# A graph-transformer kernel: transposes of late x at steps 7 and 8, the last layer's scale and shift in a chain of their own, a final norm moved behind step 29

## The chip, the cores and the metric

The kernel runs on one core of one Trainium2 chip. The metric is the device time in microseconds (us) of one execution. The times of the kernel before come from three runs, given as median with lowest and highest; the profile is one further execution with its own time. The engines are TensorE (PE, matmul; its weight loads are listed as PEld), VectorE (DVE), ScalarE (ACT), GpSimd (POOL), and SyncE (SP), which here issues most DMA transfers.

## The reference

The input x holds 16 batches of 1024 nodes with 128 features, and adj is one 1024 x 1024 matrix of zeros and ones, shared by all batches. Three transformer layers follow one another, each with 8 heads of 16 features:

```
scores = Q K^T / 4,  where adj == 0: -inf
x = layer_norm(x + softmax(scores) V Wo + bo) * ln1_g + ln1_b
x = layer_norm(x + relu(x W1 + b1) W2 + b2) * ln2_g + ln2_b
```

The last layer is a graph attention: h = x W, e[i, j] = leaky_relu(h_i . a_src + h_j . a_dst), set to -inf where adj is 0, a softmax over j, and out = layer_norm(softmax(e) h + x) * ln_gamma + ln_beta. So after the third layer's own norm and its ln2_g and ln2_b, x enters twice: through W into the nodes, and once more as the residual that the aggregation adds.

## The kernel before

**Blocks and steps.** A block is one layer of one batch. Batches are taken in groups of four (LANES): for each group all four batches' layer 0, then their layer 1, then their layer 2 (line 835), which gives 48 blocks. The last layer of a batch is no block; it runs as side work beside the blocks that follow the batch's layer 2. A block has 32 steps: two groups of heads, two halves of the queries, eight tiles of 128 keys. In this text 14.4 is step 4 of block 14. The five x buffers (four lanes and one) hold the batches in work.

**A step.** TensorE makes the scores of four heads, in two PSUM slots of 1024 columns (L545; three slots in turn). The first slot goes through ScalarE's exponential (L553) and is then multiplied by a 0/1 mask on GpSimd (L554). The second has a large negative mask added on VectorE (L557) and then goes through the exponential (L569). At the ten steps of BOTH_ON_DVE both slots take the second way. Four steps later (AHEAD) TensorE multiplies the result with v into the bank `acc` (L574). A pipeline of scores, mask, exponential and product thus runs through all 1536 steps without a break, and TensorE's order in it is fixed.

**Side work.** All else is cut into tasks: the projections of the next block (`proj_tasks`, L383, whose results ScalarE and VectorE split into two parts `hi` and `lo`, L473 to L478); the copies of these into the row layout `stack` (L530, by SP); the attention output, the norms and the two feed-forward products of the block that has just ended (`post_tasks`); the transposition of x for the next block; and `last_tasks`. For these matmuls and transposes there is a single PSUM bank, `t`.

`last_tasks` for one batch are: two transposes of x, scaled and shifted on the copy (`xt`); the node products and exponentials (`nodes`); the rows g_rows and h_rows, sent as 16 small copies by SP (`send_rows`); eight tiles of edge scores (`edges`, L769 and L774); eight aggregations (`aggregate`, L383 and L785), each with its statistics (bn_stats and bn_aggr), and with GpSimd's `normalise` after each four of them; ln_gamma and ln_beta for each half; and the two stores. The scale of x by ln2_g and its shift for the residual stand between the `nodes` tasks.

`normalise` on GpSimd is two small operations and a power on the variance (L435), then one operation per 128 rows (L441). A scale or shift of all of x by a row is one GpSimd operation over 128 x 1024 (L511, L515, L632, L798); one for half of it works on 128 x 512.

**Transposition of x.** Normally it goes by DMA (`moved`): VectorE transposes 32 x 32 blocks (L357) and SP sends them out and back (L361, L375). Where x isn't ready at step 22 of the block before, `transpose_x` with by_dma=False puts two transposes on TensorE (L345) into the next block's turn, as the tasks ("xP"). This is so for the layer-0 blocks whose x is loaded late (blocks 13 to 15, 25 to 27 and 37 to 39, whose transposes run one block earlier, and block 1). In both cases the scale and shift of x by the previous layer's norm and by `bo` follow as two GpSimd operations (in layer 0 only the shift).

**What sets the order.** Tasks stand in chains. A task has a gap to the one before it, in steps, or a step of its own from a table: AT gives the transposes' steps ("xP"), the projections' steps 5, 7, 9, 11, 17 and 19, and those of `post_tasks`. At each step `piece` goes through the chains, those with a table step first, and takes at most one task without a "*"; tasks with "*", which need no TensorE, may be taken besides. Signs such as "+x" and "-x" count buffers: a task is held until its buffer is free. `fetch`, the load of a new batch (L167, SP), needs an x buffer, which the second store of an earlier batch frees ("-x"). `need` and `need_if` run a chain forward at once when its result is asked for. TensorE, ScalarE and SP execute in the order in which the program is written; VectorE's and GpSimd's order is set by a scheduler, but `issue_after(behind["pool"])` keeps an operation behind the latest GpSimd mask.

Of the kernel before, what the change touches and what calls it, by code (L numbers as in the profile page):

```python
# [29 lines left out]
LANES = 4  # L30
FIRST = 1


AT = {"xP": (4, 6), "proj": (5, 7, 9, 11, 17, 19), "post": (13, 15, 17, 18, 21, 22, 22, 23, 24, 25, 27, 29, 31, 35, 38, 40)}
AT_V_LAST = (9, 11, 17, 19, 20, 21)
AT_FIRST = (12, 14, 16, 18, 20, 22)
T_AT = 22
STACK_AT = 24
AT_END = {3: (12, 21, 22, 24, 25, 26, 27, 28, 30, 31), 2: (8, 9, 13, 14, 15, 16, 17, 18, 20, 21)}
AHEAD = 4  # L40
BOTH_ON_DVE = (3, 7, 8, 15, 23, 24, 26, 28, 30, 31)
TILES = {"w": 8, "x": LANES + 1, "last": 2}
BLOCKED = -57344.0
# [76 lines left out]
def fast_path(ctx: ExitStack, tc: tile.TileContext, a: dict, out: bass.AP, flag):  # L120
# [18 lines left out]
    def bank():  # L139

        if head[0] or tail[0]:
            return slot()[:, :512]
        return psum.tile([P, 512], F32, tag="t", name="t", bufs=1)
# [197 lines left out]
    def transpose_half(dst, src, h, gain=None, bias=None):  # L341

        ps = bank()
        for t in range(4):
            nc.tensor.transpose(ps[:, t * P:(t + 1) * P], src[:, 4 * h + t, :], identf)  # L345
        dv, pv = dst.rearrange("p (j t e) -> p t j e", j=4, t=4), ps.rearrange("p (t j e) -> p t j e", j=4, t=4)
        with soon():
            if gain is None:
                nc.scalar.copy(dv, pv)
            else:  # L350
                nc.scalar.activation(dv, pv, AF.Identity, scale=gain, bias=bias)
# [72 lines left out]
    def normalise(n, ts):  # L424

        scalars(n, ts)
        subtract_scale(n, ts)
# [68 lines left out]
    def transpose_x(m, by_dma=True):  # L496
        b, l = blocks[m]
        x, xT = state["x", b], xt_tile("xT")
        state["xT", m] = xT
        if by_dma:  # L500
            put(moved(lambda: xT, lambda: x), ("xT", m))
        elif m == 0:
            for h in range(2):
                transpose_half(xT[:, h], x, h)
        else:
            put([(0, lambda: transpose_half(xT[:, 0], x, 0), ""), (0, lambda: transpose_half(xT[:, 1], x, 1), "")],
                ("xP", m), first=True)

        def scale():
            with tc.issue_after(behind["pool"]) if m else nullcontext():  # L510
                nc.gpsimd.tensor_mul(x, x, rows(W[l - 1]["ln2_g"]))  # L511

        def shift():
            with tc.issue_after(behind["pool"]) if m else nullcontext():
                nc.gpsimd.tensor_add(x, x, rows(W[l]["bo"]))  # L515
        if m:
            put(([(6, scale, "*")] if l else []) + [(2 if l else 6, shift, "*")], ("shifted", m))
        else:
            shift()

# [180 lines left out]
    def last_tasks(b):  # L701
# [3 lines left out]
        def xt(h):  # L705
            def run():
                w = W[L - 1]
                if h == 0:

                    s["col"] = work.tile([P, 4, NT], F32, tag="col", name="col", bufs=2)  # L710
                    s["hd"] = [work.tile([P, 4, D + 1], F32, tag="w", name="hd", bufs=TILES["w"]) for _ in range(2)]
                    s["n"] = with_stats(state["x", b])
                s["xT", h] = half_tile("xT")
                transpose_half(s["xT", h], state["x", b], h, w["ln2_gc"], w["ln2_bc"])
            return run

        def nodes(t0, t1):
            def run():
                col, ts = s["col"], slice(t0, t1)

                halves = [slice(max(t0, 4 * h), min(t1, 4 * h + 4)) for h in range(2)]
                halves = [(c, s["hd"][c.start // 4][:, c.start % 4:(c.stop - 1) % 4 + 1, :])
                          for c in halves if c.start < c.stop]
                ps = bank()
                for t in range(t0, t1):
                    by_columns(ps[:, (t - t0) * (D + 2):(t - t0 + 1) * (D + 2)],
                               s["xT", t // 4][:, t % 4 * P:(t % 4 + 1) * P], w_nodes)
                pv = ps[:, :(t1 - t0) * (D + 2)].rearrange("p (t d) -> p t d", d=D + 2)
                with soon():
                    nc.scalar.activation(col[:, 2, ts], pv[:, :, D + 1], AF.Exp, scale=NEG_SLOPE)  # L730
                    nc.scalar.activation(col[:, 0:2, ts].rearrange("p c t -> p t c"), pv[:, :, D:], AF.Exp,
                                         scale=1 - NEG_SLOPE)
                    for c, hd in halves:
                        nc.vector.tensor_mul(hd[:, :, :D], pv[:, c.start - t0:c.stop - t0, :D],
                                             col[:, 2, c, None].to_broadcast([P, c.stop - c.start, D]))
                for c, hd in halves:
                    nc.scalar.copy(hd[:, :, D], col[:, 2, c])
            return run
# [22 lines left out]
        def edges(v):  # L761
# [14 lines left out]
                                                   1.0, mask01[:, :, q:q + SLOT], op0=OP.max, op1=OP.mult)  # L776
            return run

        def aggregate(v):
            def run():  # L780
                e, ps = s["e", v], bank()
                for t in range(NT):
                    by_columns(ps[:, :D + 1], e[:, t, :], s["hd"][t // 4][:, t % 4, :], start=(t == 0), stop=(t == NT - 1))
                nc.vector.reciprocal(s["col"][:, 3, v:v + 1], ps[:, D:D + 1])
                nc.vector.scalar_tensor_tensor(s["n"][0][:, v, :], ps[:, :D], s["col"][:, 3, v:v + 1],  # L785
                                               state["x", b][:, v, :], op0=OP.mult, op1=OP.add)
                stats(s["n"], slice(v, v + 1))
                if v % 4 == 3:
                    with tc.issue_after(behind["pool"]):
                        normalise(s["n"], slice(v - 3, v + 1))  # L790
                if v == NT - 1:
                    check_range(s["col"].rearrange("p c t -> p (c t)"))
            return run

        def by_rows(op, z, v, n=NT):
            def run():
                with tc.issue_after(behind["pool"]):
                    op(z(), z(), rows(v(), n))  # L798
            return run
# [4 lines left out]
        def y(h):  # L804
            return lambda: s["n"][0][:, 4 * h:4 * h + 4, :]
# [10 lines left out]
        def two(f, g):  # L816
            def run():
# [1 line left out]
                g()  # L819
            return run  # L820

        mul, add = nc.gpsimd.tensor_mul, nc.gpsimd.tensor_add
        tasks = [(5, xt(0), "+w +last +w +w"), (1, xt(1), "+w"), (2, nodes(0, 3), ""), (2, nodes(3, 6), ""),
                 (0, by_rows(mul, x, lambda: W[L - 1]["ln2_g"]), "*"), (2, nodes(6, 8), "-w -w"),
                 (0, by_rows(add, x, lambda: ln2_b_last), "*"), (2, rows_gh, ""), (1, send_rows, "*"), (7, edges(0), "")]
        for v in range(NT - 1):
            tasks.append((2, two(edges(v + 1), aggregate(v)), ""))
            if v in (4, 6):
                tasks.append((0, by_rows((mul, add)[v // 2 - 2], y(0), lambda v=v: wl[("ln_gamma", "ln_beta")[v // 2 - 2]], 4), "*"))
        tasks += [(2, aggregate(NT - 1), ""), (2, store(0), "-last -w -w *"), (1, by_rows(mul, y(1), lambda: wl["ln_gamma"], 4), "*"),  # L830
                  (2, by_rows(add, y(1), lambda: wl["ln_beta"], 4), "*"), (3, store(1), "-x *")]
        return tasks


# [7 lines left out]
    def put(tasks, mark, chain=None, first=False, table=None):  # L842

        if chain is None:
            chain = {"due": now[0], "queue": deque()}
            chains.insert(0 if first else len(chains), chain)
        for n, task in enumerate(tasks):
            at = now[0] // (4 * NT) * 4 * NT + (table or AT[mark[0]])[n] if mark[0] in AT else None
            chain["queue"].append(task + (mark if n == len(tasks) - 1 else None, at))
        return chain  # L850

    def take(chain):

        _, f, tiles, mark, _ = chain["queue"][0]
        if any(free[t[1:]] == 0 for t in tiles.split() if t[0] == "+"):
            return False
        chain["queue"].popleft()
        f()
        for t in tiles.replace("*", "").split():
            free[t[1:]] += -1 if t[0] == "+" else 1  # L860
        done.add(mark)
        chain["due"] = now[0]
        if not chain["queue"]:
            chains.remove(chain)
        return True

    def is_due(chain):
        gap, at = chain["queue"][0][0], chain["queue"][0][4]
        return now[0] >= max(chain["due"] + gap, at or 0)

    def piece():
# [14 lines left out]
    def need_if(mark):  # L886
        if any(q[3] == mark for c in chains for q in c["queue"]):
            need(mark)
# [354 lines left out]
```

## Time and profile before

| | |
|---|---|
| Median of three runs | 3922.26 us (3920.86 to 3927.18) |
| Profiled execution | 3922.55 us |
| Its span | 3920.7 us |
| TensorE's matmuls busy | 3715.7 us |
| GpSimd busy | 3477.6 us, 2971 instructions |
| VectorE busy | 3460.5 us |
| ScalarE busy | 3296.9 us |
| Mean granted TensorE clock | 0.983 of full speed |
| One GpSimd mask (L554) | 2029 ns, 1056 of them |
| One `normalise` operation (L441) | 448 ns, 896 of them |

The span is the stretch from the first to the last recorded instruction, and the execution's own time is 1.9 us longer. Busy times are per engine and overlap. A matmul's end is modelled, so a busy TensorE need not be one at its peak speed. The lines in the next section read "start, duration, engine, line, operation, out<-in, shape, count", and square brackets give the wait before the instruction and what ended it.

### The profile page before, as it was taken

The numbers are of one execution on the slowest core, as the hardware profiler recorded it, in microseconds if no ns is written. First come the engines' busy times: TensorE is split into PE (matmuls) and PEld (weight loads), VectorE is DVE, ScalarE is ACT, GpSimd is POOL, SyncE is SP. The second block draws the span as 40 slices with busy tenths as digits, with TensorE's granted clock in tenths as the row PEclk, the third lists the DMA queues.
The fourth block names the chain that finished last, engine by engine and source line by source line (L and its number), as shares of the span: only waits on it lengthen the run. The fifth ranks groups of instructions, "written<-read, shape, count | busy, mean of one in ns | idle before, by whom it ended". The sixth has DMA issues, their size and how long they took to land.

```text
span 3920.7 us, 109674 instructions
## 1 busy us (share of the span) xinstructions
PE 3715.7 (95%) x44385; PEld 1515.1 (39%) x44385; DVE 3460.5 (88%) x5860; ACT 3296.9 (84%) x3797; POOL 3477.6 (89%) x2971
## 2 busy tenths in 40 slices
PE   7999999999989999999998999999999999999987
PEld 2333333344434333334443333333444433333346
DVE  6999999989878999998897899998898889999876
ACT  7989999977877999997777899999777789999850
POOL 5899999988978999998878899999887899999885
PEclk8999999999999999999999999999999999999998
DMA  5424334322323334332222324334232323424200
GB/s 139 113 73 103 91 81 110 76 70 70 89 63 79 98 72 110 80 95 73 72 67 76 92 66 101 95 74 100 73 82 52 88 71 93 103 71 106 63 8 21
DMA packets 245887, 319.28 MB, mean 81 GB/s; under 512 B 51072, under 2 KB 174208, under 8 KB 245376
## 3 DMA queue, kind: packets, MB, share of 16 engines
q1 hardware_dynamic: 243840, 311.52, 31.7%
q8 instruction: 353, 5.78, 0.6%
q14 instruction: 158, 1.29, 0.1%
q10 hardware_dynamic: 1536, 0.68, 0.1%
HBM read 58.53 MB, written 51.38 MB: 28 GB/s over the span
## 4 chain that ended last, share of the span: by engine, by line
POOL 46%; PE 38%; ACT 5%; DVE 5%; issue 3%; SPq 2%; DMA 1%; DVEq 0%; ACTq 0%; POOLq 0%
POOL e L554 27%; PE acc L574 13%; PE t L383 12%; PE s L545 9%; POOL x L441 7%; POOL mv L435 4%; POOL x L632 4%; ACT e L553 3%; DVE e L557 3%; ACT e L569 2%; PE s L769 2%; POOL x L798 2%; PE s L383 1%; POOL A L589 1%; SPq L530 1%
## 5 line engine op out<-in xcount | busy, mean ns | idle before, releaser
L557 DVE TENSOR_TENSOR e<-s,mask_add 128x1024 f32<-128x1024 f32 x2016 | 2377.4, 1211 | 240.3 <-PE s L545 214.5
L554 POOL TENSOR_TENSOR e<-e,mask 128x1024 f32<-128x1024 f32 x1056 | 2120.1, 2029 | 241.6 <-ACT e L553 227.8
L569 ACT ACTIVATE e<-e 128x1024 f32<-128x1024 f32 x2016 | 2110.9, 1062 | 185.2 <-DVE e L557 156.3
L574 PE MATMUL acc<-e,v 128*17 128x512 f32 x12288 | 1629.0, 602 | 78.6 <-POOL e L554 64.8
L553 ACT ACTIVATE e<-s 128x1024 f32<-128x1024 f32 x1056 | 1083.3, 1026 | 250.6 <-PE s L545 244.8
L545 PE MATMUL s<-Wq,Wk 64*128 64x512 f32 x6144 | 1196.4, 458 | 32.3 <-DVE e L557 21.1
L545 PEld LDWEIGHTS s<-Wq,Wk 64*128 64x128 f32 x6144 | 499.8, 185 | 1085.2 <-issue 388.9
L574 PEld LDWEIGHTS acc<-e,v 128*17 128x17 f32 x12288 | 205.2, 96 | 595.2 <-issue 351.1
L441 POOL TENSOR_SCALAR x<-x,mv 128x128 f32<-128x128 f32 x896 | 388.1, 448 | 19.1
L435 POOL TENSOR_TENSOR mv<-mv,half_neg 128x4 f32<-128x4 f32 (+1 forms) x179 | 214.0, 1195 | 13.6
L413 DVE BATCH_NORM_STATS2 st<-x 128x6 f32<-128x128 f32 x896 | 204.0, 281 | 7.7
L383 PE MATMUL t<-hd,ee 128*32 128x129 f32 x6656 | 205.7, 275 | 2.5 <-DVE x L420 2.4
L383 PE MATMUL t<-x1T,W 128*32 128x512 f32 x1520 | 201.9, 603 | 0.3
L774 DVE SCALAR_TENSOR_TENSOR ee<-s,mask 128x256 f32<-128x256 f32 x512 | 179.8, 413 | 23.4 <-PE s L769 23.4
L383 PEld LDWEIGHTS t<-W,hT 128*32 128x32 f32 x6080 | 170.9, 111 | 59.5 <-issue 48.4
L383 PEld LDWEIGHTS t<-hd,ee 128*32 128x32 f32 x6656 | 178.8, 110 | 16.1 <-DVE x L420 5.8
L383 PE MATMUL t<-W,hT 128*32 128x128 f32 x6080 | 184.7, 274 | 0.1
L589 POOL TENSOR_TENSOR A<-tt,recs 128x256 f32<-128x256 f32 x192 | 119.8, 624 | 49.7 <-DVE recs L588 49.6
L420 DVE TENSOR_TENSOR x<-t,x 128x512 f32<-128x512 f32 x191 | 129.1, 676 | 38.3 <-PE t L383 38.0
L649 ACT ACTIVATE hT<-t,b 128x512 f32<-128x512 f32 x190 | 130.4, 686 | 23.3 <-PE t L383 22.5
L585 DVE STREAM_TRANSPOSE tt<-acc 128x512 f32<-128x512 f32 x192 | 135.3, 705 | 0.0
L357 DVE STREAM_TRANSPOSE xb<-x 128x512 f32<-128x512 f32 x164 | 115.0, 701 | 20.1 <-POOL x L441 19.9
(145 smaller groups left out, 2531.1 us busy)
## 6 DMA issues: line engine op xcount, KB each, us to landing
Wk<-hi SPq DMA_DIRECT2D x384, 128.0 KB
Wk<-lo SPq DMA_DIRECT2D x384, 128.0 KB
Wq<-hi SPq DMA_DIRECT2D x384, 128.0 KB
Wq<-lo SPq DMA_DIRECT2D x384, 128.0 KB
tr<-xb SPq DMA_DIRECT2D x656, 64.0 KB
x1T<-tr SPq DMA_DIRECT2D x90, 256.0 KB
xT<-tr SPq DMA_DIRECT2D x74, 256.0 KB
x<-in_x_dram SPq DMA_DIRECT2D x124, 64.0 KB
```

The costliest lines, as they stand in the source:

```text
L383: nc.tensor.matmul(dst[j:j + SLOT, :], cols, rhs, start=start, stop=stop)
L413: nc.vector.bn_stats(st[:, t, :], z[:, t, :])
L435: nc.gpsimd.tensor_tensor(v, v, half_neg[:, ts], OP.pow)
L441: nc.gpsimd.tensor_scalar(z[:, t, :], z[:, t, :], mv[:, t, 0:1], mv[:, t, 1:2], op0=OP.add, op1=OP.mult)
L545: nc.tensor.matmul(ps[:, r * 512:(r + 1) * 512], k[64 * r:64 * r + 64, kt * P:(kt + 1) * P], q[64 * r:64 * r + 64, q0:q0 + 512], start=Tru ...
L553: nc.scalar.activation(ev, psv, AF.Exp, scale=HD ** -0.5)
L554: behind["pool"] = nc.gpsimd.tensor_mul(ev, ev, m).ins
L557: behind["dve"] = nc.vector.tensor_add(ev, psv, m).ins
L569: nc.scalar.activation(ev, ev, AF.Exp, scale=HD ** -0.5)
L574: nc.tensor.matmul(acc[j * SLOT:j * SLOT + HD + 1, :], v_bufs[m % 2][:, kt, 2 * j + g, :], e[:, j, :], start=first, stop=last)
L589: nc.gpsimd.tensor_mul(state["A"][:, qh, :, g, :], tt[:, :, :HD], rec[:, :, None].to_broadcast([P, 16, HD]))
L774: nc.vector.scalar_tensor_tensor(e[:, :, j * SLOT:(j + 1) * SLOT], ps.rearrange("p (k q) -> p k q", q=P)[:, :, j * SLOT:(j + 1) * SLOT], 1 ...
```

## The change

Five things are changed, all in the order of the work; each operation on the data stays.

- The table's steps for the transposes on TensorE, AT["xP"], become 7 and 8 instead of 4 and 6.
- For a block whose x is transposed by TensorE, the shift by `bo` is put 31 steps after the block's start of transposition instead of 6.
- In `last_tasks`, the scale of x by ln2_g and the shift leave the list of tasks. The second `xt` puts them into a chain ("scaled", b), ahead of the other chains. They carry the sign "~": such a task is due only at the steps 0 to 6, 22 and 23 of a block. `aggregate` asks for the chain with `need_if`. (In the old list both had a gap of 0 steps.)
- For the fourth batch of each group, the last group excepted (`late`), the normalisation of the second half leaves `aggregate` and becomes a task of its own. It, ln_gamma and ln_beta carry the sign "^": due only at the steps 30, 31 and 0 to 6. The gap before ln_beta is 1 instead of 2 there.
- `is_due` looks up these signs in the new table POOL_FREE, except in the tail after the last step; `take` strips them.

```diff
-AT = {"xP": (4, 6), "proj": (5, 7, 9, 11, 17, 19), ...
+AT = {"xP": (7, 8), "proj": (5, 7, 9, 11, 17, 19), ...
...
+POOL_FREE = {"~": (0, 1, 2, 3, 4, 5, 6, 22, 23), "^": (30, 31, 0, 1, 2, 3, 4, 5, 6)}
...
-            put(([(6, scale, "*")] if l else []) + [(2 if l else 6, shift, "*")], ("shifted", m))
+            put(([(6, scale, "*")] if l else []) + [(2 if l else 6 if by_dma else 31, shift, "*")], ("shifted", m))
...
                 transpose_half(s["xT", h], state["x", b], h, w["ln2_gc"], w["ln2_bc"])
+                if h == 1:
+                    put([(1, by_rows(mul, x, lambda: W[L - 1]["ln2_g"]), "*~"),
+                         (2, by_rows(add, x, lambda: ln2_b_last), "*~")], ("scaled", b), first=True)
...
+        mul, add = nc.gpsimd.tensor_mul, nc.gpsimd.tensor_add
+        late = b % LANES == LANES - 1 and b < B - 1
+
+        def norm(h):
+            def run():
+                with tc.issue_after(behind["pool"]):
+                    normalise(s["n"], slice(4 * h, 4 * h + 4))
+            return run
+
         def aggregate(v):
             def run():
+                need_if(("scaled", b))
                 e, ps = s["e", v], bank()
...
                 stats(s["n"], slice(v, v + 1))
-                if v % 4 == 3:
-                    with tc.issue_after(behind["pool"]):
-                        normalise(s["n"], slice(v - 3, v + 1))
+                if v % 4 == 3 and (v < NT - 1 or not late):
+                    norm(v // 4)()
...
-        mul, add = nc.gpsimd.tensor_mul, nc.gpsimd.tensor_add
         tasks = [(5, xt(0), "+w +last +w +w"), (1, xt(1), "+w"), (2, nodes(0, 3), ""), (2, nodes(3, 6), ""),
-                 (0, by_rows(mul, x, lambda: W[L - 1]["ln2_g"]), "*"), (2, nodes(6, 8), "-w -w"),
-                 (0, by_rows(add, x, lambda: ln2_b_last), "*"), (2, rows_gh, ""), (1, send_rows, "*"), (7, edges(0), "")]
+                 (2, nodes(6, 8), "-w -w"), (2, rows_gh, ""), (1, send_rows, "*"), (7, edges(0), "")]
...
-        tasks += [(2, aggregate(NT - 1), ""), (2, store(0), "-last -w -w *"), (1, by_rows(mul, y(1), lambda: wl["ln_gamma"], 4), "*"),
-                  (2, by_rows(add, y(1), lambda: wl["ln_beta"], 4), "*"), (3, store(1), "-x *")]
+        up = "*^" if late else "*"
+        tasks += [(2, aggregate(NT - 1), ""), (2, store(0), "-last -w -w *")] + [(0, norm(1), up)] * late
+        tasks += [(1, by_rows(mul, y(1), lambda: wl["ln_gamma"], 4), up), (2 - late, by_rows(add, y(1), lambda: wl["ln_beta"], 4), up),
+                  (3, store(1), "-x *")]
...
     def is_due(chain):
-        gap, at = chain["queue"][0][0], chain["queue"][0][4]
+        gap, tiles, at = chain["queue"][0][0], chain["queue"][0][2], chain["queue"][0][4]
+        for c in POOL_FREE:
+            if c in tiles and not tail[0] and now[0] % (4 * NT) not in POOL_FREE[c]:
+                return False
         return now[0] >= max(chain["due"] + gap, at or 0)
```

## The prediction

> **What bounds the kernel now.** I read the page's busy shares first, then the answers by stretch of time, then who waited for whom, then the order in time around the longest waits. A name such as 14.4 is block 14, step 4. Each step issues one mask add on VectorE (L557), two at the ten steps of BOTH_ON_DVE; counted off, their starts date every step. In a block without the last layer's work, a plain one, a turn takes 70.4 us every time. Besides the first and the last two, blocks of another kind are 11 to 15, and likewise 23 to 27 and 35 to 39, where four batches end and four begin (three "changes of group"); the block before each of these (10, 22, 34) takes 76.5, 75.0 and 76.5 us. Their stretches, with block 16 as the plain one, columns as headed:
>
> ```profile
> span 3920.7 us, 109674 instructions
> ...
> PE 3715.7 (95%) x44385; PEld 1515.1 (39%) x44385; DVE 3460.5 (88%) x5860; ACT 3296.9 (84%) x3797; POOL 3477.6 (89%) x2971
> ```
> ```profile
> core 0: us, PE busy (x) PEld busy (x) DVE busy (x) ACT busy (x) POOL busy (x), PEclk, DMA share, GB/s
> ...
> 917.20:1007.80 90.60, 90.40 (x1340) 43.81 (x1342) 82.33 (x166) 70.14 (x82) 77.01 (x73) 1.00 0.30 77
> 1007.80:1099.20 91.40, 89.16 (x1315) 42.86 (x1309) 82.97 (x168) 68.97 (x84) 75.33 (x65) 1.00 0.25 64
> 1099.20:1198.20 99.00, 85.84 (x1093) 37.20 (x1087) 77.47 (x141) 72.41 (x91) 82.10 (x71) 0.97 0.32 81
> 1198.20:1281.90 83.70, 80.35 (x986) 32.83 (x986) 73.04 (x130) 67.41 (x75) 77.05 (x70) 0.96 0.28 72
> 1281.90:1352.60 70.70, 68.63 (x706) 24.29 (x706) 65.41 (x100) 66.89 (x75) 67.69 (x56) 1.00 0.38 96
> ```
>
> TensorE is full in blocks 12 and 13; nothing can be won there by moving other engines' work. In block 14 it is idle for 13.2 us, in 15 for 3.3, with a clock under 1. Where the idle time is:
>
> ```profile
> 1108.24 2.72 SPq L812 DMA_DIRECT2D out_dram<-x  x4
> ...
> 1112.47 3.66 SPq L167 DMA_DIRECT2D x<-in_x_dram  x8
> ...
> 1117.58 1.08 PE L345 MATMUL t<-identf,x 128*128 128x128 f32 x4 [7.80 <-DMA x<-in_x_dram]
> ```
> ```profile
> 1246.42 1.74 POOL L441 TENSOR_SCALAR x<-x,mv 128x128 f32<-128x128 f32 x4
> ...
> 1248.20 0.71 DVE L357 STREAM_TRANSPOSE xb<-x 128x512 f32<-128x512 f32 x1 [3.22 <-POOL x L441]
> ...
> 1249.60 1.06 PE L383 MATMUL t<-xT,Wq 128*32 128x512 f32 x8 [1.75 <-DVE lo L477]
> ```
> ```profile
> PE t L345 <- DMA x<-in_x_dram: 21.0, 3, 7.8
> ```
>
> First fence: at 14.4 the transposes of batch 7 stand in TensorE's queue before its rows are there. The rows need the buffer that batch 2 leaves, whose store waits for POOL's last add (ends 1108.2). It happens three times, 21.0 us in all. Second fence: at 15.17 VectorE waits for POOL's normalisation, so the `lo` split behind it is late, and with it the one bank `t`. Block 14 has the same at 14.17 (1.68 and 1.10 us of TensorE).
>
> **What the Trainium skill says.** "TensorE: Matmul & The Clock Gate", Part 1, says that after an idle window of some 3.4 us the array runs at half rate until it has been busy again. The trace agrees: the stretch 1117.6 to 1122.5 has a clock of 0.63, and a product `acc` takes 1.76 us there against 1.05. The same page (section on the 16 sub-arrays) calls VectorE's, ScalarE's and GpSimd's queues strict first-in first-out: seen in the second fence, where `lo` waits though its own operands are long there. "DMA: Bandwidth & Descriptors", section "Two DMAs through the same engine are not ordered", says that the issuer has to wait for the first transfer's semaphore: SP's loads start at 1112.47, after the stores have landed, 4.2 us after their issue. "Perfetto Trace Analysis", "Identifying the Most-Contended Engine", warns that matmul busy time isn't nearness to peak; so I count idle gaps and step lengths, not busy shares.
>
> **The change part by part.** I compared the two programs as built, engine by engine.
>
> 1. Transposes at 7 and 8 (nine pairs act; block 1's keep their place). Steps 4 and 6 come free, so batch 2's last chain runs two steps earlier: its last aggregation stands at 13.30 instead of 14.0. On POOL this puts add of `bo`, normalisation, `ln_gamma`, `ln_beta` between the masks of 13.29 and 14.0, where POOL is idle for 9.59 us. From 1089.0: `bo` 2.40; statistics of an aggregation at 13.30 are there at 1095.2 (this is when 13.30's are now); normalisation 0.24+0.23+1.04+4x0.45 and gaps, 3.6; two half rows at 1.29: end 1101.6, 6.6 us before now. From that end to the first transpose it takes 9.4 us (1108.2 to 1117.6), so x is there at 1111.0. Step 14.7 starts after 10.8 us (14.0 to 14.3) and three steps of some 2.8 us, at 1118. Cover: 7 us. The wait goes: 21.0 us. With it goes the cold clock: 4.9 us x 0.37 = 1.8, thrice, say 5. Mask 14.0 comes 2 us later (1103.6), needed at 1108.7: nothing. SP's sixteen row copies of `stack`, queued behind the load, move forward with it.
> 2. The same move takes 0.81 us at 13.31 (the aggregation waiting for the bank): 2.4.
> 3. POOL in block 14: from 1099.9 to the normalisation at 1151.2 it is busy 44.2 us (51.3 less 5.93 and 1.16 idle). The parts that leave (3.6, 2.6, `bo` 2.4) make 8.6, so 35.6, while TensorE needs about 40 for these steps without its wait. POOL is then in time at 14.17: 3 x (1.68+1.10) = 8.3. The adds `bo` land at 12.29, 13.29, 14.29, in idle gaps of 5.6, 9.6 and 3.6 us: nothing.
> 4. Late norm of batch 3 (7, 11): 3.6+2.6 = 6.2 us of POOL leave 15.6 to 15.11. Steps 15.17 to 15.20 take 11.9 us, in block 16 7.7: 4.2 gained, 12.6 in all.
> 5. They come back at 15.29 to 16.0, where POOL has no gap (1277.9 to 1288.2). Mask 16.0 ends 5.0 later, at 1289.2, needed at 1289.2; mask 16.1 6.2 later, at 1292.5, needed at 1290.95: 1.6 us of wait. Gaps of 0.68, 1.01 and 0.20 take back 1.9; The store of this half moves behind 32 copies on SP, to 16.3; beta ends at about 1290.5 and nothing that waits stands behind it. 2.7 are left at 16.17 beside TensorE's shift, with 0.9 spare, so VectorE waits about 2 us; by 15.17 (3.2 cost 4.2) that is 2.6. Together 4.2 per change of group, 12.6 lost; bounds 0 (all absorbed) and 20 (wait of 3.2 and a cold clock).
> 6. Scale and shift of x. In block 10 one row (2.40) leaves POOL before 10.25's mask, for which TensorE waits 2.50 at 10.29. But the sixteen `g_rows`, `h_rows` copies leave SP one by one until 821.85, and the first edges at 11.0 start at 822.77; in block 23 they already wait 2.01 for them. TensorE would only arrive earlier at that wait: nothing; bounds 7 gained, 5 lost (cold clock before the edges). At 11.22 the three rows stay as they are, at 11.0 and 12.0 the add meets idle POOL. The change adds a wait here: the first aggregation reads x after the add at 11.0 (mask 11.0 ends at 824.8, the add at 827.2) and now starts its read on VectorE at 830.2: 3 us to spare; behind it on VectorE stand the mask adds, and TensorE's scores wait for those.
> 7. Bank `t`: the transpose at 8 is one step before the projection at 9. Between lie a score and a product (0.7+1.05), the copy takes 0.58: 1 us for all nine, bounds 0 and 9.
> 8. End: at 47.22 TensorE waits 2.44 for a mask behind five rows on POOL; one leaves. 2 gained, bounds 0 and 4.
>
> Sum: 21.0 + 5 + 2.4 + 8.3 + 12.6 - 12.6 + 0 - 1 + 2 = 37.7. The profiled execution took 3922.55 us (span 3920.7 and 1.9 around it), so 3884.9; the median of the runs is 0.3 lower and the sum is no better than that. I say 3885.
>
> **The rivals.**
> A, the above: 3885, by itself 3874 to 3898.
> B, POOL's lag in block 16 is absorbed (part 5 costs nothing): 3885 - 12.6 = 3872. For it: masks there have 5 us to spare; against: no gap in POOL's line.
> C, only the wait for x goes: part 3 gains nothing and part 5 and 7 cost their bounds, 37.7 - 8.3 - 7.4 - 4 = 18: 3904. For it: POOL is busy for 30.4 of 31.0 us from 1129 to 1160, so it may stay late whatever leaves.
> D, the change doesn't do what it says: x comes as late after step 7 as after step 4: all the rest cancels, 3920. It needs the store 7 us later than worked out; against: its inputs move two steps.
> E, slower: POOL does not recover from the late norm. A plain block leaves POOL 70.40 - 67.65 = 2.75 us idle. If the lag of 6.2 is not paid in block 16 but returns as a stall of 4.2 in each block after, it outweighs the gains (50.3 without part 5) from four blocks on (4 x 12.6 = 50.4); five give 3935. Against: now the same 6.2 in block 15 are paid within it, block 16 is back at 70.7.
>
> **How the numbers follow.** A 0.52, B 0.17, C 0.19, D 0.05, E 0.07. Faster by over 0.2% (7.8 us, about what runs of this kernel can tell from no change) are A, B, C: 0.88; within it D: 0.05; slower E: 0.07. The range leaves out D and E, takes in B with a gain of part 6 (3865) and C with its loss (3909): 3864 to 3911.
>
> **What would show it.** Right: L345 waits for no DMA of x in blocks 14, 26, 38, and block 14 lasts 85 to 90 us instead of 99; steps 15.17 to 15.20 take about 8 us; block 16 is longer than 70.7, with `xb` waiting for POOL at 16.17; at 11.0 the edges wait for `g_rows`; blocks 17 to 21 stay at 70.4. Wrong: a wait for x at 14.7, a projection at step 9 waiting for ScalarE's copy, plain blocks over 71, or steps 14.17 and 15.17 as long as now.

## The result and the profile after

The changed kernel takes 3895.60 us (median of four runs, 3895.29 to 3896.76) against 3921.56 us before (3920.77 to 3927.18): a ratio of 0.9931, 95% interval 0.9914 to 0.9948. The profiled execution took 3895.71 us, its span 3893.8 us, 26.9 us less than the span before. The forecast was 37.7 us less.

The answer by stretch of time, block by block from 10 to 16 (columns as in the prediction; line numbers of the changed kernel are one higher at first and some thirteen higher in the last layer's tasks: L545 is now L546, L769 is L773):

```profile
745.80:818.40 72.60, 71.08 (x778) 26.16 (x776) 67.17 (x105) 69.70 (x88) 67.80 (x57) 1.00 0.33 85
818.40:920.20 101.80, 94.85 (x1355) 45.42 (x1356) 83.61 (x171) 70.56 (x88) 79.13 (x74) 0.95 0.26 67
920.20:1015.10 94.90, 92.16 (x1340) 44.67 (x1342) 82.73 (x165) 70.10 (x82) 79.35 (x74) 0.98 0.28 73
1015.10:1105.20 90.10, 89.62 (x1324) 43.08 (x1313) 82.92 (x169) 69.74 (x85) 78.11 (x71) 1.00 0.25 65
1105.20:1191.10 85.90, 82.91 (x1087) 36.40 (x1085) 77.08 (x142) 71.13 (x90) 79.44 (x66) 1.00 0.36 93
1191.10:1269.60 78.50, 77.85 (x986) 32.63 (x985) 72.72 (x130) 66.98 (x75) 71.27 (x63) 1.00 0.28 73
1269.60:1344.30 74.70, 68.69 (x706) 23.98 (x706) 65.55 (x100) 67.42 (x75) 73.39 (x63) 1.00 0.38 97
```

Block 14 went from 99.1 to 85.9 us and 15 from 83.7 to 78.5, as forecast. Two blocks grew: 11 from 94.2 to 101.7, with a clock of 0.95 instead of 1.00, and 12 from 90.6 to 94.9, with 0.98 instead of 1.00. Block 11 of the kernel before:

```profile
823.00:917.20 94.20, 90.83 (x1355) 44.31 (x1356) 83.45 (x169) 70.55 (x88) 79.23 (x74) 1.00 0.27 72
```

Block 16 grew by 4 us, and block 10 fell from 76.5 to 72.6.

Over the three changes of group, from step lengths counted off in both traces (us; differences of the sums):

| blocks | before, first group | after, first group | three groups together | forecast, by part |
|---|---|---|---|---|
| 10 and 11 (22, 23; 34, 35) | 170.7 | 174.3 | +6.2 | 0 (6) |
| 12 (24; 36) | 90.6 | 94.9 | +12.9 | +1 (7) |
| 13 (25; 37) | 91.4 | 90.1 | -3.9 | -2.4 (2) |
| 14 (26; 38) | 99.1 | 85.9 | -38.6 | -34.3 (1 and 3) |
| 15 (27; 39) | 83.7 | 78.5 | -16.0 | -12.6 (4) |
| 16 (28; 40) | 70.7 | 74.7 | +13.0 | +12.6 (5) |
| 46 and 47 with the end | | | +0.5 | -2 (8) |
| block 2 and the start | | | -0.9 | |

The sum is -26.8. Of the first row, block 10 and its like gained 10.1 and block 11 and its like lost 16.3. The last two rows are no finding: block 2 took 74.8 us in one profiled execution of the changed kernel and 76.4 in another. Blocks 17 to 21 stay at 70.4.

Where the gain of block 14 sits is read in TensorE's order of time at 14.7. The transposes of batch 7 run without a wait:

```profile
1121.09 0.66 PE L346 MATMUL t<-identf,x 128*128 128x128 f32 x4
```

And where the losses sit: at 11.0 TensorE stands still for 3.92 us, and what follows takes 1.91 us for a product that takes 1.05 elsewhere. First TensorE, then SP's queue in the same stretch:

```profile
818.16 0.32 PE L773 MATMUL s<-g_rows,h_rows 4*128 4x128 f32 x1
822.41 1.08 PE L773 MATMUL s<-g_rows,h_rows 4*128 4x128 f32 x7 [3.92 <-DMA h_rows<-parts]
824.57 1.91 PE L575 MATMUL acc<-e,v 128*17 128x512 f32 x8
```
```profile
810.51 0.79 SPq L760 DMA_DIRECT2D g_rows<-parts  x1
...
820.65 0.59 SPq L761 DMA_DIRECT2D h_rows<-parts  x1
```

The waits, added up over the whole span, for the kernel before and then for the changed one:

```profile
PE s L769 <- DMA h_rows<-parts: 6.3, 3, 5.2
```
```profile
PE s L773 <- DMA h_rows<-parts: 18.4, 6, 5.1
```

At 12.10 the aggregation waits for the bank `t`, which VectorE's split `lo` still has to read. First TensorE's aggregation, then VectorE before it:

```profile
947.11 3.04 PE L384 MATMUL t<-hd,ee 128*32 128x129 f32 x64 [2.21 <-DVE lo L474]
```
```profile
943.59 1.22 DVE L558 TENSOR_TENSOR e<-s,mask_add 128x1024 f32<-128x1024 f32 x1
944.94 1.42 DVE L778 SCALAR_TENSOR_TENSOR ee<-s,mask 128x256 f32<-128x256 f32 x4
946.27 0.68 DVE L474 TENSOR_TENSOR lo<-t,hi 128x512 fp32r<-128x512 f32 x1
```

VectorE is hardly idle there; it does four edge operations first. The aggregation of 64 matmuls, 1.98 us elsewhere, takes 3.04 at a lower clock.

### The profile page after: what moved, and what is told of

The parts are those of the page before. It is cut to its first block, busy times and chain, and to the rows that moved or that the text cites. A ratio compares the mean times of both kernels' runs of the same rounds, so it can differ in the third digit from the quotient of the medians.

```text
span 3893.8 us, 109695 instructions
## 1 busy us (share of the span) xinstructions
PE 3715.9 (95%) x44385; PEld 1515.9 (39%) x44385; DVE 3460.6 (89%) x5860; ACT 3293.8 (85%) x3797; POOL 3477.7 (89%) x2971
## 3 DMA queue, kind: packets, MB, share of 16 engines
q14 instruction: 158, 1.29, 0.1%
## 4 chain that ended last, share of the span: by engine, by line
POOL 47%; PE 38%; ACT 6%; DVE 4%; issue 3%; SPq 1%; DMA 1%; ACTq 0%; DVEq 0%; POOLq 0%
POOL e L555 28%; PE acc L575 13%; PE t L384 12%; PE s L546 9%; POOL x L442 7%; POOL x L633 4%; POOL mv L436 4%; ACT e L554 3%; ACT e L570 2%; DVE e L558 2%; PE s L773 2%; POOL x L811 1%; PE s L384 1%; POOL A L590 1%; POOL mv L435 1%
## 5 line engine op out<-in xcount | busy, mean ns | idle before, releaser
L546 PE MATMUL s<-Wq,Wk 64*128 64x512 f32 x6144 | 1196.4, 458 | 29.5 <-DVE e L558 17.2
L546 PEld LDWEIGHTS s<-Wq,Wk 64*128 64x128 f32 x6144 | 498.8, 185 | 1080.9 <-issue 383.5
L650 ACT ACTIVATE hT<-t,b 128x512 f32<-128x512 f32 x190 | 130.6, 687 | 13.2 <-PE t L384 12.2
L358 DVE STREAM_TRANSPOSE xb<-x 128x512 f32<-128x512 f32 x164 | 115.1, 702 | 10.1 <-POOL x L442 9.8
```

Source lines behind the costliest of these rows:

```text
L546: nc.tensor.matmul(ps[:, r * 512:(r + 1) * 512], k[64 * r:64 * r + 64, kt * P:(kt + 1) * P], q[64 * r:64 * r + 64, q0:q0 + 512], start=Tru ...
```

## The experiments

Each is one edit on the changed kernel, or several together where it says so. The kernel before took 3929.33, 3921.97 and 3928.95 us beside the three sets of runs, so medians are read against the run of before of their own set, and the reading goes by the blocks of the profiled execution. Most blocks that an edit leaves alone agree to 0.2 us, but a single block can differ by up to 1.7 us between executions (block 12 took 93.3 us instead of 94.9 in a run whose edit doesn't touch it; the last section shows where such a step comes from). The differences below are sums over the three groups, against the kernel before, to be set beside the last table.

**Transposes back at 4 and 6.**

```diff
-AT = {"xP": (7, 8), ...
+AT = {"xP": (4, 6), ...
```

> The changed kernel with the late transposes back at steps 4 and 6, all else kept. Theory (the move carries the gain in the change of group, and brings the new wait in block 12 with it): block 14 goes from 85.9 back to 97 to 99 us, its transposes wait about 7 to 8 us for the load of x again; block 13 goes from 90.1 to about 91.4; block 12 goes back from 94.9 to 90.6; so about 3 x (12.5 + 1.3 - 4.3) = +28, near 3924. Rival (the scale and shift in a chain of their own and the later shift by bo free GpSimd, and this alone brings batch 2's store and so x earlier): the wait for x stays under 4 us, block 14 under 93, the whole under 3910.

Measured: 3917.52 us, 0.9968 of before (0.9956 to 0.9981); span 3916.2. Block 12 is back (-0.2), so is 13 (0.0), and 14 stands at -10.5 instead of -38.6. The wait is there again:

```profile
PE t L346 <- DMA x<-in_x_dram: 20.3, 3, 7.2
```

So the move of the transposes carries 28.1 of block 14's gain and all of block 13's, and it also causes the whole loss in block 12; the rival (x comes earlier without the move) falls. Block 14 was expected back at 97 to 99 us and came to 95.6, 95.4 and 94.9, since 14.17 had fallen from 5.6 to 2.3 us. In this run `bo` is gone from GpSimd ahead of 14.17, and the scale and shift of batch 3 have moved from 14.9 and 14.12 into TensorE's wait at 14.4.

**`lo` ahead of the edge operations on VectorE.**

```diff
                 for j in range(4):
                     q = v // 4 * 512 + j * P + t
-                    nc.vector.scalar_tensor_tensor(e[:, :, j * SLOT:(j + 1) * SLOT], ...
+                    with tc.issue_after(low[now[0] - 1]) if now[0] - 1 in low and not tail[0] else nullcontext():
+                        nc.vector.scalar_tensor_tensor(e[:, :, j * SLOT:(j + 1) * SLOT], ...
```

> The changed kernel with one order added on VectorE: the four edge operations of a step stand behind the split lo of the projection one step before. Theory (at 12.10 TensorE's aggregation waits 2.2 us for lo only because VectorE has it behind four edge operations, 1.6 us of them, and the clock falls after it): the wait is gone, blocks 12, 24 and 36 take 90.5 to 91.5 us instead of 94.9, together -10 to -13, so 3883 to 3886. Rival (ScalarE gives hi too late, since it copies the transposed half of step 8 first, so that lo can't start earlier by more than a few tenths): blocks 12, 24, 36 stay at 94 or more, 3894 to 3896. A third way: the edge operations become the late ones, and blocks 11 and 13 grow by what block 12 loses.

Measured: 3891.00 us, 0.9898 (0.9881 to 0.9914); span 3889.7. Blocks 12, 24, 36 take 91.8 us each: +3.6 instead of +12.9. Blocks 10, 11 and 13 to 16 keep their differences to within 0.4 us. VectorE at 12.10, then TensorE:

```profile
946.60 0.68 DVE L474 TENSOR_TENSOR lo<-t,hi 128x512 fp32r<-128x512 f32 x1
947.20 1.41 DVE L779 SCALAR_TENSOR_TENSOR ee<-s,mask 128x256 f32<-128x256 f32 x4
```
```profile
947.43 1.98 PE L384 MATMUL t<-hd,ee 128*32 128x129 f32 x64 [0.66 <-DVE lo L474]
```

The aggregation is back at 1.98 us. The cause is VectorE's order, not ScalarE's: `hi` was there in time for a `lo` right after the mask add. The rest of the wait (0.66) can be part of the 1.2 us that block 12 keeps.

**Transposes at 6 and 7.**

```diff
-AT = {"xP": (7, 8), ...
+AT = {"xP": (6, 7), ...
```

> The changed kernel with the late transposes at steps 6 and 7 instead of 7 and 8. Theory (the price of step 8 is that lo of the projection at 9 falls behind the edge operations of 12.10; one step more between them puts it ahead): blocks 12, 24, 36 fall from 94.9 to 91 to 92, and if x is there by then, block 14 stays within 1 us of 85.9: -9 to -12 in all, like the run with lo put first. The prediction's other number, a cover of 7 us for x at step 7, would leave 3 us at step 6. Rival (the cover was less; in the changed kernel the semaphore before the first transpose at 14.7 is passed at about 1120.7, 0.4 us before it runs): blocks 14, 26, 38 wait 1 to 3 us for the load and grow by 1 to 5 each, which takes back a part or all of it.

Measured: 3902.01 us, 0.9927 (0.9910 to 0.9943); span 3899.2. One half of the expectation is wrong, the other right. Block 12 stays at 94.9 us, with VectorE and TensorE at 12.10 as in the changed kernel:

```profile
946.45 1.40 DVE L778 SCALAR_TENSOR_TENSOR ee<-s,mask 128x256 f32<-128x256 f32 x4
947.78 0.68 DVE L474 TENSOR_TENSOR lo<-t,hi 128x512 fp32r<-128x512 f32 x1
```
```profile
948.60 2.79 PE L384 MATMUL t<-hd,ee 128*32 128x129 f32 x64 [2.21 <-DVE lo L474]
```

That the second transpose stands only one step ahead of the projection isn't what puts `lo` behind. Why the scheduler prefers the edge operations after these two placements and not after 4 and 6 stays open. But block 14 takes 86.1 us, and the transposes at 14.6 wait for nothing, 13.6 us after the block's start where at 14.7 it is 15.9. So x has more to spare than the rival held, at least 2.3 us. It isn't the prediction's 7 us either: in the trace of the changed kernel the last of the eight loads of x lands at 1118.35 by its semaphore, 2.7 us ahead of the transposes at 1121.09.

**Stack copies of blocks 10, 22 and 34 at step 21.**

```diff
-                    if at == (24 if m == 0 else STACK_AT):
+                    if at == (24 if m == 0 else 21 if m % 12 == 10 and m < 46 else STACK_AT):
```

> The changed kernel with the sixteen copies of stack in blocks 10, 22 and 34 issued at step 21 instead of 24, ahead of the transposed x1's copies, so that SP comes to the g_rows and h_rows copies some 4 us earlier. Theory (what the scale and shift gain in block 10 is lost again at 11.0, where TensorE waits 3.9 us for the last row copy on SP's queue and then runs at a lower clock for about 2 us): the wait at 11.0 falls under 1 us, blocks 11, 23, 35 take 95 to 98 instead of 101.7, 100.7, 102.5, together -11 to -18: 3878 to 3885. Rival (SP is not the bound: the rows are waited for through their own making or landing, or the second half of x1 comes too late now and TensorE waits at 10.27 instead): block 10 or 11 gives it back, 3893 to 3897.

Measured: 3881.96 us, 0.9878 (0.9861 to 0.9894); span 3876.7. Blocks 10 and 11 with their like go from +6.2 to -12.1, all else stays. At 11.0:

```profile
819.22 0.66 PE L773 MATMUL s<-g_rows,h_rows 4*128 4x128 f32 x8
```

There is no wait, and the clock is 1.00 from 813 to 829 us. SP's queue was the bound, as the theory said. The rival may be right in one small point: TensorE waits 1.52 us at 10.27, ahead of the product with the transposed x1, whose copies now stand behind the stack's. That these copies are the reason isn't shown, since the trace names ScalarE for the wait. The block takes 73.6 instead of 72.6 us, while 22 and 34 show nothing.

**Scale and shift back among the `nodes` tasks.**

```diff
-                if h == 1:
-                    put([(1, by_rows(mul, x, ...), "*~"), (2, by_rows(add, x, ...), "*~")], ("scaled", b), first=True)
...
-                 (2, nodes(6, 8), "-w -w"), (2, rows_gh, ""), ...
+                 (0, by_rows(mul, x, ...), "*"), (2, nodes(6, 8), "-w -w"),
+                 (0, by_rows(add, x, ...), "*"), (2, rows_gh, ""), ...
```

> The changed kernel with the scale and shift of x for the last layer back between the nodes tasks, without the chain and without the rule on its steps. Theory (in blocks 10 and 11 the chain gains at 10.29 what is lost again at 11.0 on SP's queue, and more): block 10 back to 75 to 76.5, block 11 to 94 to 96, 22 and 23, 34 and 35 likewise: 2 to 6 us less than the changed kernel in these blocks together; block 14 within 1 us of 85.9, since its own scale and shift of batch 3 move by a few steps only; block 47's steps 22 and 23 back to 6.7 and 3.1. Rival (the chain is needed for the move of the transposes: with the scale at 13.0 and 14.0 GpSimd is late for batch 2's last norm): block 14 over 88.

Measured: 3897.12 us, 0.9913 (0.9896 to 0.9929); span 3895.8. Blocks 10 and 11 and their like stand at +3.1 instead of +6.2. Block 10 and its like take 75.0, 76.7 and 77.8 us and block 11 and its like 98.6, 95.7 and 95.8: longer before the rows, shorter after. Block 14 takes 86.3 us, so the chain isn't needed for the transposes' gain. So the chain of its own gains nothing in these blocks; here they are 3.1 us shorter without it. The half of the +6.2 that stays isn't due to the chain.

**Late norm taken back.**

```diff
-        late = b % LANES == LANES - 1 and b < B - 1
+        late = False
```

> The changed kernel with batch 3's (7's, 11's) second half normalised in its aggregation again, and ln_gamma and ln_beta one and two steps later, all else kept. Theory (6.2 us of GpSimd's work cost 4 us in block 15 where they stood and 4 us in block 16 where they went: the late norm by itself is worth 0 to 4 us in all): block 15 goes from 78.5 back to 83.5 or so, block 16 from 74.7 to 70.7, the same in 27 and 28, 39 and 40: within 4 us of the changed kernel. Rival (block 15 gains from the other parts too, the shift by bo above all, so that the late norm only costs): blocks 15, 27, 39 stay under 80 and blocks 16, 28, 40 fall to 70.7, together -8 to -12.

Measured: 3901.79 us, 0.9946 (0.9929 to 0.9962); span 3904.7. Block 15 and its like go from -16.0 to +1.3, block 16 and its like from +13.0 to 0.0. So the late norm is the whole gain in the one and the whole loss in the other: 17.3 against 13.0, 4.3 us in all. The rival falls.

**ln_gamma and ln_beta of the late norm at step 2 of blocks 17 and 18.**

```diff
-        tasks += [(1, by_rows(mul, y(1), ...), up), (2 - late, by_rows(add, y(1), ...), up),
+        tasks += [(1 + 35 * late, by_rows(mul, y(1), ...), up), (2 + 30 * late, by_rows(add, y(1), ...), up),
```

> The changed kernel with batch 3's ln_gamma and ln_beta moved on by one and two blocks (step 2 of blocks 17 and 18), while its normalisation stays at 15.30. Theory (block 16 takes 74.7 instead of 70.7 because 6.2 us of GpSimd's work arrive where it has no gap, and a plain block has 1.6 us of gaps at its steps 3 to 7, where one half row of 1.29 fits): block 16 falls to 71 to 73, blocks 17 and 18 stay within 0.5 of 70.4, together -6 to -11: 3885 to 3890. Rival (the loss is fixed by the normalisation at the seam, 3.6 us in front of the masks of 16.0 and 16.1): block 16 stays at 74 or more, 3894 to 3897. Rival (GpSimd never catches up what is added to it, in whatever block): the 4 us only move to blocks 17 and 18.

In the changed kernel GpSimd's order at this seam is:

```profile
1270.55 1.04 POOL L436 TENSOR_TENSOR mv<-mv,half_neg 128x4 f32<-128x4 f32 x1
1271.69 1.74 POOL L442 TENSOR_SCALAR x<-x,mv 128x128 f32<-128x128 f32 x4
1273.51 1.29 POOL L811 TENSOR_TENSOR x<-x,ln_gamma 128x512 f32<-128x512 f32 x1
1274.76 2.03 POOL L555 TENSOR_TENSOR e<-e,mask 128x1024 f32<-128x1024 f32 x1
1276.73 1.30 POOL L811 TENSOR_TENSOR x<-x,ln_beta 128x512 f32<-128x512 f32 x1
```

Measured: 3893.85 us, 0.9906 (0.9890 to 0.9923); span 3890.0. Block 16 and its like go from +13.0 to +6.3 (72.7, 72.2, 72.8 us), and blocks 17 and 18 show no difference. So GpSimd's gaps in blocks 17 and 18 take one half row each, and half of the seam's loss came from the two half rows; the other half stays with the normalisation.

**Shift by `bo` at gap 6 again.**

```diff
-            put(... [(2 if l else 6 if by_dma else 31, shift, "*")], ("shifted", m))
+            put(... [(2 if l else 6, shift, "*")], ("shifted", m))
```

In this kernel the transposed x of these layer-0 blocks has `bo` added already, which the reference doesn't do (layer 0's `bo` is zero in these inputs).

> The changed kernel with the shift by bo of the blocks transposed by TensorE at gap 6 again instead of 31. The prediction's part 3 (GpSimd's lag before 14.17 is paid by whatever leaves: norm 3.6, half rows 2.6, bo 2.4, of which the wait of 3.2 needs about half): block 14 stays within 1 us of 85.9, step 14.17 at 3.7 or less. Rival (the shift is what counted: with the transposes at steps 4 and 6 and the shift at 31, 14.17 was 2.3 us already, though the norm and the half rows were still in block 14): step 14.17 goes back to 5 us or more and block 14 to 87.5 to 89, likewise 26 and 38: +5 to +9 in all.

Measured: 3946.79 us, 1.0063 (1.0046 to 1.0079); span 3944.9. Neither theory: 49.7 us longer than the changed kernel in the same set, in steps that neither had named. Block 13 goes from -3.9 to +16.6 and block 14 from -38.6 to -13.6. TensorE at 14.7, then GpSimd:

```profile
1135.29 1.11 PE L346 MATMUL t<-identf,x 128*128 128x128 f32 x4 [7.47 <-POOL x L516]
```
```profile
1128.30 3.97 POOL L555 TENSOR_TENSOR e<-e,mask 128x1024 f32<-128x1024 f32 x2
...
1132.90 2.34 POOL L516 TENSOR_TENSOR x<-x,bo 128x1024 f32<-128x1024 f32 x1
```

A task at step 6 is now written into the program ahead of the transposes at 7 and 8, and both touch the same x. So the transposes wait for GpSimd's addition, which stands behind the masks. With the transposes at 4 and 6 the shift came after them at the same gap. The later gap is a condition of the later transposes, and the prediction missed that: it costed the shift as 2.4 us of GpSimd's time and looked for a gap where it would fit. Whether the shift or the norm pays at 14.17 can't be read here, since TensorE waits ahead of that step.

**Three edits together** (`lo` first, stack at 21, half rows spread).

> Three edits at once on the changed kernel: lo ahead of the edge operations on VectorE, the stack copies at step 21 in blocks 10, 22 and 34, ln_gamma and ln_beta of the late norm at step 2 of blocks 17 and 18. If the three losses are independent, as their blocks suggest, the blocks add up: 12, 24, 36 at 91.8, 11, 23, 35 at 94.1 to 95.7, 16, 28, 40 at 72.2 to 72.8, together -9.3 - 19.4 - 6.5 = -35 from the changed kernel, a span of about 3859. If they draw on the same slack (an earlier TensorE arrives earlier at the next wait, on GpSimd at 11.29 or on SP at the loads), less than two thirds of it: over 3870.

Measured: 3862.39 us, 0.9849 (0.9832 to 0.9865); span 3859.6, against 3859 expected. Blocks 10 and 11 with their like stand at -12.4, 12 at +3.6, 16 at +5.6, each about what its own edit gave: the three losses are independent.

**A fourth edit: no scale at steps 22 and 23 for the second batch of a group.**

```diff
-POOL_FREE = {"~": (0, 1, 2, 3, 4, 5, 6, 22, 23), ...
+POOL_FREE = {"~": (0, 1, 2, 3, 4, 5, 6, 22, 23), "`": (0, 1, 2, 3, 4, 5, 6), ...
...
+                    up = "*`" if b % LANES == 1 and b < B - LANES else "*~"
```

> The run with three edits, and for the second batch of a group (1, 5, 9) the scale and shift of x only at steps 0 to 6, which takes one row of 2.40 us from GpSimd between 11.22 and 11.29. Theory (TensorE waits 2.5 us at 11.29 for a mask behind three rows on GpSimd, and its clock falls after it): the wait goes, blocks 11, 23, 35 fall from 94.0, 95.6, 95.9 by 2 to 4 each: -6 to -12 from the run with three edits, a span of 3848 to 3854. Rival (the scale at 12.0 and the shift at 12.2 come too near to the first aggregation at 12.6, which waits for them, and the masks behind them are late): block 12 gives it back, 3858 to 3862.

Measured: 3855.46 us, 0.9808 (0.9792 to 0.9825); span 3853.4. Blocks 11, 23 and 35 take 92.4 us each, and 12 keeps its 91.8 to 92.0. In the changed kernel and in this one, at 11.29:

```profile
909.76 1.46 PE L575 MATMUL acc<-e,v 128*17 128x512 f32 x8 [2.49 <-POOL e L555]
```
```profile
903.99 1.05 PE L575 MATMUL acc<-e,v 128*17 128x512 f32 x8 [0.29 <-POOL e L555]
```

**A fifth edit: the late normalisation cut in two.** The statistics and two row tiles stay at 15.30, the other two go to block 17, the half rows to 18 and 19.

```diff
...
-        tasks += [...] + [(0, norm(1), up)] * late
+        tasks += [...] + [(0, norm_first, up), (36, norm_rest, up)] * late
-        tasks += [(1 + 35 * late, by_rows(mul, y(1), ...), up), ...
+        tasks += [(1 + 30 * late, by_rows(mul, y(1), ...), up), ...
```

> The run with four edits, and the late normalisation cut in two: the statistics and two of four row tiles (2.5 us) at 15.30, the other two (0.9 us) at step 2 of block 17, ln_gamma and ln_beta in blocks 18 and 19. Theory (each 1 us less on GpSimd at the seam is 1 us less of lag at 16.17, of which about 1.9 us is waited for): blocks 16, 28, 40 fall from 72.2 to 71.0 to 71.8, and 17 stays at 70.4: -1 to -4 in all. Rival (block 16's rest comes from 1.5 us of statistics, not from the row tiles): no difference over 1 us.

Measured: 3854.07 us, 0.9804 (0.9787 to 0.9820); span 3855.2. Block 16 and its like take 71.3, 71.3 and 71.4 us, 2.9 less together, as expected; the whole is the same as with four edits within what these runs can tell. By spans both are 1.0% shorter than the changed kernel (3853.4 and 3855.2 against 3893.8), and by the ratios some 2% shorter than the kernel before.

**The changed kernel once more**, in the second set of runs.

> The changed kernel once more, unaltered, beside the runs of this call, since the kernel before took 7.8 us longer beside the last four runs than beside the first. If the chip adds the same to both, this run stands at 0.993 of before, and its blocks are as in the first profile to within 0.5 us, except the load waits in blocks 2 and 47.

Measured: 3897.14 us, 0.9935 (0.9918 to 0.9952). Its blocks 3 to 45 are those of the first profile to within 0.6 us; block 2 took 76.4 us.

## Why the prediction was right or wrong

The time lies in the range, and the signs of the large parts are right: case A's mechanism, at a smaller size, inside case A's own range of 3874 to 3898. That the sum missed by only 10.8 us is in part luck. Two steps, parts 6 and 7, lost 18.1 us more than forecast, and parts 1 to 4 gained 9.2 more; the rest is the end and the start.

Parts 1 to 3, the late x, its clock, 13.31 and 14.17: forecast 36.7, measured 42.5 in blocks 13 and 14. The wait of 21.0 us is gone, and taking the move back brings 20.3 of it again. The mechanism is the one forecast, but its margin was smaller: x landed 13.2 us after the start of block 14 where 11.8 was worked out, and the transposes came after 15.9 where step 14.7 was put at 18.8, so the cover was 2.7 us, not 7.

Part 3 by itself was too large: 14.17 fell from 5.6 to 3.7 us, 5.6 us in the three groups where 8.3 was forecast. Its working set 35.6 us of GpSimd's work against some 40 of TensorE's. GpSimd's work in block 14 of the changed kernel, up to the normalisation at 14.17, is 38.40 us of 39.00:

```profile
1105.20:1144.20 39.00, 37.54 (x425) 14.91 (x427) 34.68 (x58) 35.72 (x50) 38.40 (x31) 1.00 0.29 76
```

The two half rows, which the sum let leave, still stand in block 14, at 1105.83 and 1107.19 (2 x 1.29 us), and VectorE still waits for the normalisation:

```profile
1147.74 0.71 DVE L358 STREAM_TRANSPOSE xb<-x 128x512 f32<-128x512 f32 x1 [1.33 <-POOL x L442]
```

With the transposes at 4 and 6, 14.17 was 2.3 us, which fits GpSimd catching up during TensorE's wait ahead of it; no run takes the causes apart.

Parts 4 and 5, the late norm: forecast -12.6 and +12.6, measured -16.0 and +13.0. The run without it shows that the late norm is the cause of both. Block 16 pays at 16.5, where TensorE waits for the mask of 16.1, and at 16.17, as forecast:

```profile
1280.06 1.05 PE L575 MATMUL acc<-e,v 128*17 128x512 f32 x8 [1.32 <-POOL e L555]
```
```profile
1310.59 0.71 DVE L358 STREAM_TRANSPOSE xb<-x 128x512 f32<-128x512 f32 x1 [1.89 <-POOL x L442]
```

Rival B, that block 16 absorbs it, falls; so does E: blocks 17 to 21 are at 70.4.

Part 6, "TensorE would only arrive earlier at that wait: nothing", is the first wrong step. Its first half is right: the wait at 10.29 is down from 2.50 to 0.58 us, and 11.0 has one of 3.92. But the earlier arrival isn't worth nothing, since the clock fell after the new wait. Between 822.4 and 828.9 us it was 0.54, which is 6.5 x 0.46 = 3.0 us lost. The prediction had this as the lower bound (5 lost) and chose the middle; measured, 6.2 were lost, beyond the bound. The run with the stack copies ahead shows the place: 18.3 us between the two orders of SP's queue.

Most of the 6.2 is clock. Half of the time in which TensorE worked at half clock is an estimate of what the clock cost. By the traces' clock records that is 8.0 us for blocks 10 and 11 and their like before, 13.2 in the changed kernel and 11.5 without the chain. So 5.2 of the +6.2 is clock, and so is all of the +3.1 that stays without the chain; the chain's own share, about 3 us, lies in the range of one or two such stretches and is not well settled.

Part 7, "1 us for all nine, bounds 0 and 9", is the second. It looked at the right bank but at the wrong engine: it asked how long ScalarE's copy holds `t` and didn't ask where the scheduler would put `lo` on VectorE. It cost 12.9 us, beyond the bound, of which 9.3 go by order alone.

Part 8, 2 gained at the end: 46 and 47 differ by +0.5 here and by up to 2.8 between runs with the same end; nothing can be said of it.

The rivals C (part 3 gains nothing) and D (x as late after step 7) fall with 14.17 and the load's wait, though C's loss in part 7 came true and more. What no case held is that the later shift is needed for the move: costed as a load on GpSimd at nothing, it is worth some 50 us as an order between two users of x.

## What to carry to other kernels

When a step is taken out of the way of a full engine, look up which wait it meets next, and price that wait with the clock that follows: here the 3.8 us won in block 10 became a wait of 3.92 us in block 11 and 3.0 us of low clock. Where a scheduler orders an engine, read every engine's order in the program as built, not only those of the engines that the change names: one split behind four small operations cost 9.3 us over three places. A task that writes a tensor in place is an ordering constraint first and a load second; moving its reader without it can cost more than the move brings.

## What the runs showed of the hardware

Waits of 2.2 to 2.5 us sometimes lower TensorE's clock and sometimes don't. The same wait at 11.29 (2.50 and 2.49 us, for the same mask) ran on at full clock in the kernel before and was followed by half clock in the changed one. By stretch of time, the kernel before and then the changed kernel:

```profile
906.18:909.59 3.41, 1.36 (x16) 0.40 (x16) 1.25 (x2) 1.90 (x3) 3.41 (x3) 1.00 0.31 88
909.59:913.01 3.42, 3.33 (x32) 0.96 (x27) 2.33 (x3) 2.69 (x3) 3.42 (x3) 1.00 0.02 5
```
```profile
906.86:910.27 3.41, 0.92 (x12) 0.20 (x12) 2.11 (x3) 2.77 (x4) 3.41 (x3) 1.00 0.46 114
910.27:913.69 3.42, 3.42 (x20) 0.78 (x12) 0.00 (x0) 0.72 (x2) 3.42 (x3) 0.50 0.02 5
```

The Trainium skill, "TensorE: Matmul & The Clock Gate", Part 1, describes the window over which TensorE's activity is watched as free-running, some 3.4 us long. The clock records of these fourteen traces agree. After the first 200 us and up to block 47 they hold 134 stretches at half clock; within one execution all begin on one grid of 3.41 us, and each is one, two or three grid lengths long. The stretches above are cut on that grid. The page's table puts half rate after an idle window. Here the window needn't be idle throughout: from block 2 to 46, a window at full clock in which TensorE was busy for less than 1.3 us was always followed by half clock, one with more than 2.4 us never, and in between both occur.

So a wait shorter than the window counts if enough of it falls into one window. In the changed kernel all 2.49 us did. In the kernel before the wait ran from 905.73 to 908.23, so 0.45 us of it fell into the window ahead. Where it falls differs from execution to execution. A wait of this size is therefore worth its length, or its length and about 1.7 us more, half of one window: in the 5.8 us after the wait of 2.21 us at 12.10 the clock was 0.71.
